# A graph layer's own-node product, moved from the node values into the PSUM sum of its edges

## The chip, the core and the metric

The kernel runs on one core of a Trainium2 chip. A core has five engines with instruction streams of their own, which wait for each other through semaphores: TensorE (PE; its weight loads are shown as PEld), VectorE (DVE), ScalarE (ACT), GpSimd (POOL) and SyncE (SP), which here only issues DMAs. Matrix products are written to PSUM; all other tiles lie in SBUF. Transfers between SBUF and DRAM are done by 16 DMA engines; SP, ACT and POOL issue them. The metric is the device time of one execution in microseconds, lower is better. Where times are compared, the median of several executions is meant.

## What is computed

Four residual steps on 6250 nodes of 256 features, each on a layer norm of x, with 106250 edges sorted by destination: a graph layer with edge attributes, an attention layer with four experts of which two count for each node, a second graph layer, and a last layer of four experts with a shared one. The change is in the second graph layer (D = 256, projection P = 128):

```python
def _L1_gnn_ref(x, edge_vals, Wp, bp, W1, b1, W2, b2, src, dst):
    MU = 2.0
    h = relu(x @ Wp.T + bp)                    # 6250 x 128: a node's own projection
    hp = h ** MU
    msgs = edge_vals[:, None] * hp[src]        # 106250 x 128
    agg = segment_sum(msgs, dst, num_segments=N)
    agg = agg ** (1.0 / MU)
    return h @ W1.T + b1 + agg @ W2.T + b2     # 6250 x 256

x = x + _L1_gnn_ref(_layernorm(x), edge_weight, ...)   # the second graph layer
x = x + _L1_ffn_ref(_layernorm(x)[None], ...)[0]       # the last experts
```

So a node gets the product of its own projection (`h @ W1.T`) and the product of the root of its edges' sum (`agg @ W2.T`). The first needs nothing but the node itself; the second needs `hp` of all its neighbours.

## The kernel before

Nodes are held in 49 tiles of 128 (a tile's number is `w` or `t`; 128 nodes lie on the 128 partitions). `x_all` and `b_all`, each 128 x 49 x 256 float32, stay in SBUF for the whole kernel: x_all is the residual stream, b_all holds what each layer needs of a node, mostly its normed values transposed (features on partitions), in two halves of 128 columns a tile. All products are float32; a product is made of two passes on PE for each factor pair, and each pass has a weight load and a matmul record.

The kernel has these stages: node products of the first graph layer (to about 270 us), its edges (to about 1675 us), the attention together with the first experts (to 3037 us), and the second graph layer's edges together with the last experts (to the end).

**The attention stage.** A loop over 80 groups of 8 columns of edges (`for k in range(NA + 5)`, line 2113) mixes several sequences by hand. In each turn POOL gathers the attention rows of group k (`fetch`), PE and DVE score, weigh and sum those of the groups before (`score`, `weigh`, `spread_out`, `add_up`), and between these parts `slot()` advances two more things: `experts1`, the first experts (products `ph` and `py`, gelu on ACT, L1607), and `steps`, in which the node values of the second graph layer are made.

`node_values(ws)` (line 1949) is a generator for two tiles at a time. It starts when their attention gates and the experts' outputs (loaded back from DRAM by L1944) are there. Its steps: sum the four experts into x_all (L1956) and take the layer norm's mean and scale (L1961 to L1970); write the normed values (ACT, L1976), and add the biases b1 + b2 to x_all (DVE, L1980); transpose them into b_all (PE L1987, ACT L1988); multiply by wpt, and relu into a tile `ht` (ACT, L1994), which is h transposed, 128 projections on the partitions by 128 nodes; then transpose `ht` back (PE, L1998) into one half of a PSUM tile `py`, multiply `ht` by w1t into the other half (L1999), square the first half on ACT (L2001), add the second to x_all on DVE (L2002), and store the square to `hp_dram` (SP, L2003). The PSUM pool `psy` has two buffers. They are shared by the transposes, the products with wpt, the back-transposes and the second products of `experts1`, so each new one waits until the last reader of the tile two before is done. After the loop, turns without attention work go on until all 49 tiles are made.

**The last stage.** The gathers of `hp` need the whole of `hp_dram`. A loop over 139 groups of six edge tiles (line 2451) does for group k: POOL gathers the rows of group k + 4 (`fetch`, six buffers `hg`), DVE makes the 96-wide selection with the edge weights (`weights_of`, L2390), PE adds the group up into the PSUM tile `pe` of the block of nodes (`add_up`, L2411). A block is four node tiles (ten such, then three of two and three of one); its tile has two buffers. When a block's last edge tile is in, `roots(b)` takes the square root of its sums on ACT (L2423), and `end_of2` is begun for one of its tiles every other turn: the product with w2t into a PSUM tile `pt` (pool `psm`, one buffer), its addition to x_all (L2229), the layer norm, a transpose into b_all (L1085, L1086) and the product with the gate's weights. When a block is through, `gates2` and `experts2` route it and run the experts; `advance` moves them by one to three steps a turn.

Weights of the last stage are loaded at its beginning, by SP, into the pool `w8`. The order in which the loops issue their work is not quite the order in which each engine runs it: the framework that builds the program schedules ready instructions of neighbouring turns into one another. For example the first loads of the last stage (L2174, 3024 us) stand on SP's queue before the last stores of hp (L2003, 3037 us). Each engine then runs its list strictly in order.

Helpers record under their own lines: a `mm` product is L1091, `transposed` L1085 and L1086, a gather L1104; the tile names tell them apart (`py<-w1t,ht` is the product that the change is about, `pt<-w2t,gt` the one of the edges).

Of the kernel before, what the change touches and what calls it, by code (L numbers as in the profile page):

```python
# [8 lines left out]
F32 = mybir.dt.float32  # L9
I32 = mybir.dt.int32  # L10
AF = mybir.ActivationFunctionType
# [5 lines left out]
P = 128  # L17
# [824 lines left out]
def kernel(ctx: ExitStack, tc: tile.TileContext, a: dict, out: bass.AP):  # L842
# [10 lines left out]
    N, D = a["x"].shape  # L853
# [63 lines left out]
    with ExitStack() as fast:  # L917
# [22 lines left out]
        def bcast_row(pool, name, ap):  # L940

            n = ap.shape[0]
            t = pool.tile([P, n], F32, name=name)
            SY.dma_start(t, bass.AP(tensor=ap.tensor, offset=ap.offset, ap=[[0, P], [1, n]]))
            return t
# [20 lines left out]
        if T1 > C1:  # L966
            V.memset(flat.bitcast(I32)[:, C1:T1], 2**24)
            n = E1 - C1 * P
# [119 lines left out]
        def mm(dst, lhs, rhs, n=2):  # L1088

            for c in range(n):  # L1090
                TE.matmul(dst, lhs(c), rhs(c), start=c == 0, stop=c == n - 1)  # L1091
# [565 lines left out]
        with (  # L1657
# [270 lines left out]
            bp = w6.tile([P, 1], F32, name="bp")  # L1928
            with nc.allow_non_contiguous_dma(reason="a bias, one element a partition"):
                SY.dma_start(bp, a["L1_gnn_bp"].rearrange("(c p) -> p c", p=P))  # L1930
            w1t = w6.tile([P, D], F32, name="w1t")
            SY.dma_start(w1t, a["L1_gnn_W1_T"])
            b1 = bcast_row(w6, "b1", a["L1_gnn_b1"])
            V.tensor_add(b1, b1, bcast_row(n6, "xn", a["L1_gnn_b2"]))
            ys = {}
            done = {"gates": 0, "loads": 0, "sums": 0, "begun": 0}

# [11 lines left out]
            def node_values(ws):  # L1949

                mv = n6.tile([P, 2, 2], F32, name="ln_mv")
                rs = n6.tile([P, 2], F32, name="ln_rs")
                off = n6.tile([P, 2], F32, name="off")
                for i, w in enumerate(ws):
                    for e in range(X):
                        V.scalar_tensor_tensor(  # L1956
                            x_all[:, w, :], ys.pop((w, e)), gate[:, w, e : e + 1], x_all[:, w, :],
                            op0=OP.mult, op1=OP.add,
                        )
                    st = n6.tile([P, 6], F32, name="ln_st")  # L1960
                    V.bn_stats(st, x_all[:, w, :])  # L1961
                    V.bn_aggr(mv[:, i, :], st)
                    V.tensor_scalar(rs[:, i : i + 1], mv[:, i, 1:2], EPS, None, op0=OP.add)
                    done["sums"] += 1
                    yield w == ws[-1]
                n = len(ws)
                SC.activation(rs[:, 0:n], rs[:, 0:n], AF.Sqrt)
                yield False
                V.reciprocal(rs[:, 0:n], rs[:, 0:n])
                V.scalar_tensor_tensor(  # L1970
                    off[:, 0:n], mv[:, 0:n, 0], -1.0, rs[:, 0:n], op0=OP.mult, op1=OP.mult
                )
                xns, hts = {}, {}
                for i, w in enumerate(ws):
                    xns[w] = n6.tile([P, D], F32, name="xn")
                    SC.activation(  # L1976
                        xns[w], x_all[:, w, :], AF.Identity, bias=off[:, i : i + 1],
                        scale=rs[:, i : i + 1],
                    )
                    V.tensor_add(x_all[:, w, :], x_all[:, w, :], b1)  # L1980
                    yield False
                begun.remove(ws)
                for w in ws:
                    pt = psy.tile([P, 2, D], F32, name="py")[:, 0, :]
                    for c in range(2):
                        at = slice(c * P, (c + 1) * P)
                        TE.transpose(pt[:, at], xns[w][:, at], ident)  # L1987
                    SC.activation(b_all[:, w, :], pt, AF.Copy)  # L1988
                    yield False
                for w in ws:  # L1990
                    ph = psy.tile([P, 2, D], F32, name="py")[:, 0, 0:P]
                    mm(ph, lambda c: wpt[:, c, :], lambda c: b_all[:, w, c * P : (c + 1) * P])
                    hts[w] = n6.tile([P, P], F32, name="ht")
                    SC.activation(hts[w], ph, AF.Relu, bias=bp)  # L1994
                    yield False
                for w in ws:
                    py = psy.tile([P, 2, D], F32, name="py")
                    TE.transpose(py[:, 0, 0:P], hts[w], ident)  # L1998
                    mm(py[:, 1, :], lambda c: hts[w], lambda c: w1t, 1)  # L1999
                    hp = n6.tile([P, PD], F32, name="hp")  # L2000
                    SC.activation(hp, py[:, 0, 0:P], AF.Square)  # L2001
                    V.tensor_add(x_all[:, w, :], x_all[:, w, :], py[:, 1, :])  # L2002
                    SY.dma_start(nodes(hp_dram)[:, w, :], hp)  # L2003
                    yield False

# [158 lines left out]
        with (  # L2164
# [7 lines left out]
        ):  # L2172
            w2t = wp.tile([P, D], F32, name="w2t")
            SY.dma_start(w2t, a["L1_gnn_W2_T"])  # L2174
            gw = load_rows(wp, "gw", a["L1_ffn_gW"])
            gb = bcast_row(wp, "gb", a["L1_ffn_gb"])
            sw1 = load_rows(wp, "sw1", a["L1_ffn_sW1"])
# [45 lines left out]
            def end_of2(b, i, root):  # L2223


                w = blocks[b][0] + i
                pm = psm.tile([P, D], F32, name="pt")
                mm(pm, lambda c: root[:, i, :], lambda c: w2t, 1)
                V.tensor_add(x_all[:, w, :], x_all[:, w, :], pm)  # L2229
                st = wk.tile([P, 6], F32, name="ln_st")  # L2230
                V.bn_stats(st, x_all[:, w, :])
                mv = wk.tile([P, 2], F32, name="ln_mv")
                V.bn_aggr(mv, st)
                rs = wk.tile([P, 1], F32, name="ln_rs")
                V.tensor_scalar(rs, mv[:, 1:2], EPS, None, op0=OP.add)
                SC.activation(rs, rs, AF.Sqrt)
                yield
                V.reciprocal(rs, rs)
                off = wk.tile([P, 1], F32, name="off")
                V.tensor_scalar(off, mv[:, 0:1], rs, -1.0, op0=OP.mult, op1=OP.mult)  # L2240
                xn = wk.tile([P, D], F32, name="xn")
                SC.activation(xn, x_all[:, w, :], AF.Identity, bias=off, scale=rs)
                yield
                transposed(psm, b_all[:, w, :], xn)
                yield
                pg = psm.tile([P, D], F32, name="pt")
                mm(pg[:, 0:NX], lambda c: b_all[:, w, c * P : (c + 1) * P], lambda c: gw[:, c, :])
                V.tensor_add(logits(b)[:, i * NX : (i + 1) * NX], pg[:, 0:NX], gb)
# [169 lines left out]

            def roots(b):
                n = blocks[b][1]  # L2420
                root = wk.tile([P, BT, P], F32, name="gt")[:, 0:n, :]
                pe = sums.pop(b)[:, 0 : n * P].rearrange("p (w k) -> p w k", k=P)
                SC.activation(root, pe, AF.Sqrt)  # L2423
                return [(b, i, root) for i in range(n)]
# [116 lines left out]
```

## Time and profile before

| | us |
|---|---|
| median of 8 runs | 4353.14 (4332.4 to 4371.82) |
| the profiled execution | 4340.81 |
| its span, first to last instruction | 4338.9 |
| attention stage in which node values are made | 2110 to 3037 |
| first gather of hp, last gather of hp | 3040.8, 4257 |
| PE, DVE, ACT, POOL busy, share of the span | 81%, 50%, 32%, 52% |
| granted TensorE clock, mean | 0.869 |

The tables of groups name a line, an engine, the tiles written and read, the shape and the count; then the busy time in us and the mean of one in ns; behind the second bar the time for which the engine sat idle just before, and what ended most of it. "x98" for a product of 49 tiles means two passes each. "Issue" is idle time in which the profile shows no wait; "remote" is a wait that ended with a signal that the profile cannot attribute. A matmul's record begins when PE takes it up, and its end is modelled, so the signal of a matmul can reach the other engines well after its recorded end. The granted clock is the share of full speed that the throttle left to PE.

### The profile page before, as it was taken

The page shows a single profiled execution, that of the slowest core. Times are in us where ns is not written, and L with a number is a line of the kernel's source. Part 1 is how long each engine was busy: PE and PEld are TensorE (multiplying, and loading weights), DVE is VectorE, ACT ScalarE, POOL GpSimd, SP SyncE. Part 2 cuts the span into 40 slices and gives each one's busy share as a digit, 9 for nine tenths or more (in the row PEclk, how much of TensorE's full clock was granted, in tenths as well). Part 3 has the DMA queues.
Part 4 walks back from the last instruction along what each step waited for, and adds up shares of the span by engine and source line. Part 5 has one row for each costly group of instructions (what it writes and reads, how often), then busy time and mean ns, then how long its engine had stood idle before and what let it go on. Part 6 is the DMA issues. An engine that isn't in the chain of part 4 may idle for free.

```text
span 4338.9 us, 57680 instructions
## 1 busy us (share of the span) xinstructions
PE 3501.4 (81%) x20063; PEld 2713.6 (63%) x20063; DVE 2185.1 (50%) x6292; ACT 1397.3 (32%) x2752; POOL 2246.3 (52%) x2367
## 2 busy tenths in 40 slices
PE   8788889998899997788888889878336866877788
PEld 3566666676666665676777777666234644555566
DVE  9788674443333333565646465656123333333445
ACT  4333333333333332333433443445001111211123
POOL 0455455555555554444544444541666666666651
PEclk9999999999999998899999999989556676766778
DMA  5455445554545443232433233333111111111210
GB/s 156 128 157 160 136 148 161 159 159 148 155 151 160 148 148 82 69 79 67 112 70 106 67 105 71 101 84 91 50 45 51 51 50 50 51 50 50 53 46 25
DMA packets 342929, 428.52 MB, mean 99 GB/s; under 512 B 139174, under 2 KB 246453, under 8 KB 342630
## 3 DMA queue, kind: packets, MB, share of 16 engines
q1 hardware_dynamic: 245174, 244.98, 19.0%
q0 software_dynamic: 89408, 178.08, 16.7%
q8 instruction: 162, 2.65, 0.3%
q10 hardware_dynamic: 8048, 1.68, 0.2%
q14 instruction: 137, 1.12, 0.1%
HBM read 382.05 MB, written 42.49 MB: 98 GB/s over the span
## 4 chain that ended last, share of the span: by engine, by line
PE 60%; another core or an unknown queue 12%; issue 11%; DVE 9%; ACT 5%; POOL 2%; DMA 2%; SPq 0%; ACTq 0%; DVEq 0%; POOLq 0%
PE ph L1091 26%; PE py L1091 9%; PE pt L1085 6%; PE pe L1443 5%; PE pe L2411 5%; PE po L1771 3%; PE pt L1091 3%; POOL hg L1104 1%; DMA rb<-low_dram 1%; PE pa L1708 1%; ACT L1607 1%; DVE order L1237 1%; ACT hh L1607 1%; DVE key L1240 1%
## 5 line engine op out<-in xcount | busy, mean ns | idle before, releaser
L1104 POOL DMA_INDIRECT yg<-y_dram,src x882 | 842.1, 955 | 804.9 <-ACT h L1422 321.1
L1104 POOL DMA_INDIRECT hg<-hp_dram,src x831 | 786.0, 946 | 451.9 <-issue 229.2
L1104 POOL DMA_INDIRECT sg<-gat_dram,src x640 | 612.7, 957 | 647.8 <-DVE px L1743 308.5
L1091 PE MATMUL ph<-w1b,et 128*128 128x256 f32 x3528 | 874.6, 389 | 32.0 <-issue 30.2
L1091 PEld LDWEIGHTS ph<-w1b,et 128*128 128x128 f32 x3528 | 654.2, 196 | 127.7 <-issue 52.3
L1417 DVE TENSOR_TENSOR yg<-ph,yg 128x512 f32<-128x512 f32 x441 | 300.1, 687 | 459.2 <-PE ph L1091 170.8
L2411 PEld LDWEIGHTS pe<-eq,hg 128*128 128x128 f32 x2036 | 373.8, 261 | 203.1 <-issue 125.5
L2411 PE MATMUL pe<-eq,hg 128*128 128x96 f32 (+15 forms) x2036 | 383.3, 341 | 139.2 <-issue 66.1
L1091 PE MATMUL py<-w,hh 128*128 128x256 f32 x1568 | 412.0, 401 | 65.2 <-ACT hh L1607 31.6
L2390 DVE TENSOR_SCALAR eq<-px,dst,ew 128x96 f32<-128x96 f32 x831 | 261.5, 369 | 324.2 <-remote 115.0
L1091 PE MATMUL ph<-b_all,w 128*128 128x256 f32 (+1 forms) x1600 | 407.0, 394 | 4.2 <-issue 4.1
L1086 ACT ACTIVATE et<-pt 128x512 f32<-128x512 f32 x441 | 259.4, 595 | 393.2 <-PE pt L1085 191.8
L1091 PEld LDWEIGHTS py<-w,hh 128*128 128x128 f32 x1568 | 297.9, 198 | 121.3 <-issue 41.0
L1422 ACT ACTIVATE h<-yg 128x512 f32<-128x512 f32 x441 | 275.7, 629 | 222.4 <-DVE yg L1417 164.4
L1091 PEld LDWEIGHTS ph<-b_all,w 128*128 128x128 f32 x1600 | 303.7, 199 | 44.3 <-issue 7.3
L1085 PE MATMUL pt<-ident,ea 128*128 128x128 f32 x1764 | 286.6, 283 | 37.6 <-issue 19.4
L1443 PE MATMUL pe<-h,eq 128*32 128x257 f32 x3168 | 256.5, 386 | 59.0 <-issue 30.6
L1607 ACT ACTIVATE hh<-ph,b 128x256 f32<-128x256 f32 (+1 forms) x400 | 166.0, 467 | 378.9 <-remote 116.8
L1085 PEld LDWEIGHTS pt<-ident,ea 128*128 128x128 f32 x1764 | 215.6, 147 | 109.4 <-issue 65.8
L1771 PE MATMUL po<-pp,B 128*128 128x240 f32 (+10 forms) x1280 | 265.5, 348 | 12.1 <-issue 8.4
L1771 PEld LDWEIGHTS po<-pp,B 128*128 128x128 f32 x1280 | 224.6, 197 | 29.0 <-issue 11.5
L1443 PEld LDWEIGHTS pe<-h,eq 128*32 128x32 f32 x3168 | 104.1, 109 | 190.2 <-issue 91.9
(331 smaller groups left out, 4324.2 us busy)
## 6 DMA issues: line engine op xcount, KB each, us to landing
ea<-in_edge_attr_dram SPq DMA_DIRECT2D x147, 768.0 KB
y<-y SPq DMA_DIRECT2D x196, 128.0 KB
w<-in_L_ffn_W_dram SPq DMA_DIRECT2D x48, 512.0 KB
y<-ys SPq DMA_DIRECT2D x96, 256.0 KB
rb<-low_dram SPq DMA_DIRECT2D x80, 256.0 KB
yg<-y_dram,src POOLq DMA_INDIRECT x882
hg<-hp_dram,src POOLq DMA_INDIRECT x831
sg<-gat_dram,src POOLq DMA_INDIRECT x640
```

What stands on the lines that cost most here:

```text
L1085: TE.transpose(pt[:, c, :], src[:, c * P : (c + 1) * P], ident)
L1086: SC.activation(dst, pt.rearrange("p c k -> p (c k)"), AF.Copy)
L1091: TE.matmul(dst, lhs(c), rhs(c), start=c == 0, stop=c == n - 1)
L1104: GP.indirect_dma_start(out=dst, out_offset=None, in_=table[0:NP, :], in_offset=IndirectOffsetOnAxis(ap=idx, axis=0),)
L1237: V.max(out=top, in_=key)
L1417: V.tensor_add(y, ph, y)
L1422: SC.activation(h[:, j : j + 2, 0:D], y, AF.Relu)
L1443: TE.matmul(sums[w][b * Q : (b + 1) * Q, :], eq[k][:, j, at], h[:, i * NT + j, :], start=g == 0 and j == NT - 1, stop=g == last_of[b] and ...
L1607: SC.activation(hidden[u][:, f, :n, :], ph[:, f - f0, :n, :], AF.Gelu, bias=b1[:, e, f : f + 1],)
L1771: TE.matmul(po.rearrange("p b v -> p (b v)"), B[:, j, :], pp[:, j, 0:n, :].rearrange("p b v -> p (b v)"), start=half == 0 and j == 0, stop ...
L2390: V.tensor_scalar(equals[k][:, j, :], lanes[:, 0:NW], dst_of[:, t : t + 1], ew[:, t : t + 1], op0=OP.is_equal, op1=OP.mult,)
L2411: TE.matmul(sums[b][:, lo - t0 * P : hi - t0 * P], hg[:, j, :], eq[:, j, lo - n0 : hi - n0], start=False, stop=after >= (t0 + n) * P,)
```

## The change

The node's own product leaves `node_values`. The relu writes h transposed into the first half of the tile's b_all, which the product with wpt has just read, where it stays. At the end of the second graph layer, `end_of2` makes one PSUM sum of two factors, b_all's first half by w1t and the edges' root by w2t, and adds that to x_all. The biases b1 + b2 are no longer added tile by tile in `node_values` but block by block in `roots`, in one wide DVE addition with the bias row broadcast over the block's tiles. w1t and the bias rows are loaded with the weights of the last stage instead of those of the attention.

```diff
@@ weights of node_values
-            w1t = w6.tile([P, D], F32, name="w1t")
-            SY.dma_start(w1t, a["L1_gnn_W1_T"])
-            b1 = bcast_row(w6, "b1", a["L1_gnn_b1"])
-            V.tensor_add(b1, b1, bcast_row(n6, "xn", a["L1_gnn_b2"]))
@@ node_values
-                xns, hts = {}, {}
+                xns = {}
...
-                    V.tensor_add(x_all[:, w, :], x_all[:, w, :], b1)
...
-                    hts[w] = n6.tile([P, P], F32, name="ht")
-                    SC.activation(hts[w], ph, AF.Relu, bias=bp)
+
+                    SC.activation(b_all[:, w, 0:P], ph, AF.Relu, bias=bp)
...
-                    TE.transpose(py[:, 0, 0:P], hts[w], ident)
-                    mm(py[:, 1, :], lambda c: hts[w], lambda c: w1t, 1)
+                    TE.transpose(py[:, 0, 0:P], b_all[:, w, 0:P], ident)
                     hp = n6.tile([P, PD], F32, name="hp")
                     SC.activation(hp, py[:, 0, 0:P], AF.Square)
-                    V.tensor_add(x_all[:, w, :], x_all[:, w, :], py[:, 1, :])
                     SY.dma_start(nodes(hp_dram)[:, w, :], hp)
@@ weights of the last stage
             SY.dma_start(w2t, a["L1_gnn_W2_T"])
+            w1t = wp.tile([P, D], F32, name="w1t")
+            SY.dma_start(w1t, a["L1_gnn_W1_T"])
+            b12 = bcast_row(wp, "b12", a["L1_gnn_b1"])
+            V.tensor_add(b12, b12, bcast_row(wp, "b2", a["L1_gnn_b2"]))
@@ end_of2
-                mm(pm, lambda c: root[:, i, :], lambda c: w2t, 1)
+                mm(
+                    pm, lambda c: (b_all[:, w, 0:P], root[:, i, :])[c],
+                    lambda c: (w1t, w2t)[c],
+                )
                 V.tensor_add(x_all[:, w, :], x_all[:, w, :], pm)
@@ roots
                 n = blocks[b][1]
+                at = slice(blocks[b][0], blocks[b][0] + n)
+                V.tensor_add(
+                    x_all[:, at, :], x_all[:, at, :],
+                    b12[:, None, :].to_broadcast([P, n, D]),
+                )
                 root = wk.tile([P, BT, P], F32, name="gt")[:, 0:n, :]
```

## The prediction

> **What bounds the kernel now.** I read the busy times in stretches first, because the change takes work out of one stage (the attention, in which the second graph layer's node values are made, 2110 to 3037 us) and puts it into another (the second graph layer with the last experts, from 3037 us on). Columns: stretch, its length, busy us of PE, PE's weight loads, DVE, ACT and POOL, then the granted clock, DMA share, GB/s.
>
> ```profile
> 2110.00:3037.00 927.00, 792.18 (x4849) 675.54 (x4849) 551.65 (x1437) 406.70 (x723) 404.00 (x420) 0.94 0.36 89
> ...
> 3178.00:4257.00 1079.00, 769.73 (x3029) 567.91 (x3030) 400.78 (x1502) 190.13 (x337) 690.08 (x730) 0.69 0.19 50
> ```
>
> The attention is PE's stage: 85% busy at a clock of 0.94. In the last stage PE is 71% busy at 0.69, and POOL issues a gather for each of 831 edge tiles; here two engines can be the bound. Second view, groups of instructions of the attention, for what the change takes away there, with PE's waits behind it; third, the same for the last stage.
>
> ```profile
> L1091 PE MATMUL py<-w1t,ht 128*128 128x256 f32 x98 | 31.1, 402 | 0.0
> ...
> L1987 PE MATMUL py<-ident,xn 128*128 128x128 f32 x98 | 21.0, 299 | 22.6 <-DVE x_all L2002 11.8 <-ACT xn L1976 4.0 <-ACT b_all L1988 3.0
> L1998 PE MATMUL py<-ident,ht 128*128 128x128 f32 x49 | 14.9, 305 | 23.0 <-DVE x_all L2002 22.0 <-issue 0.6 <-DVE ys L1623 0.3
> ...
> L2002 DVE TENSOR_TENSOR x_all<-x_all,py 128x256 f32<-128x256 f32 x49 | 20.3, 416 | 16.5 <-issue 9.2 <-ACT hp L2001 7.0
> L1980 DVE TENSOR_TENSOR x_all<-x_all,b 128x256 f32<-128x256 f32 x49 | 20.3, 419 | 10.7 <-ACT xn L1976 6.9 <-issue 3.6
> ```
>
> ```profile
> L1104 POOL DMA_INDIRECT hg<-hp_dram,src x831 | 786.0, 946 | 451.9 <-issue 229.2 <-remote 102.5 <-PE pe L2411 81.9
> ...
> L1091 PE MATMUL pt<-w2t,gt 128*128 128x256 f32 x98 | 44.0, 542 | 39.3 <-ACT b_all L1086 25.0 <-issue 13.8 <-DVE px L2248 0.3
> ```
>
> A product of 128x256 is two passes: 31.1/49 = 0.63 us a node in the attention, 44.0/49 = 0.90 us in the last stage. A gather takes 0.95 us and 0.30 of issue, 1.25 in all, 7.5 for a group of six; 831 x 1.25 = 1039 us, and POOL spends 1216 (3041 to 4257). What lies between is POOL waiting for a gather buffer that PE has yet to read. In POOL's order of time:
>
> ```profile
> 3647.26 0.95 POOL L1104 DMA_INDIRECT hg<-hp_dram,src  x1 [3.49 <-remote]
> ...
> 3654.76 0.95 POOL L1104 DMA_INDIRECT hg<-hp_dram,src  x1 [0.30 <-DMA hg<-hp_dram,src]
> ...
> 3664.47 0.95 POOL L1104 DMA_INDIRECT hg<-hp_dram,src  x1 [2.51 <-PE pt L1085]
> ...
> 3671.97 0.94 POOL L1104 DMA_INDIRECT hg<-hp_dram,src  x1 [0.30 <-DMA hg<-hp_dram,src]
> ```
>
> Each line is the first gather of a group: one group runs on at 7.5 us, the next waits some 3 us for PE. Counting along the stage, 71 of 138 groups go at POOL's pace. So PE's work counts there, but not all of it.
>
> **The change, part by part.** In the attention it removes, a node, one product (PE) and two additions on DVE; x_all is then last touched by the layer norm, and a PSUM tile `py` is free when ACT has squared it (L2001), not when DVE has added it (L2002).
>
> (a) 49 products, 31.1 us of PE. The stage is 85% PE, so I take 0.85 x 31 = 26 us off. Ends: 0, if something else were the limit, and 31.
>
> (b) PE's waits for L2002, 22.0 + 11.8 = 33.8 us. They do not all go. One of the longest:
>
> ```profile
> 2224.24 0.28 ACT L2001 ACTIVATE hp<-py 128x128 f32<-128x128 f32 x1 [0.65 <-ACT hh L1607]
> ...
> 2227.09 0.56 DVE L1725 TENSOR_TENSOR za<-pa,A 128x384 f32<-128x384 f32 x1 [4.40 <-remote]
> ...
> 2227.57 0.41 DVE L2002 TENSOR_TENSOR x_all<-x_all,py 128x256 f32<-128x256 f32 x1
> ...
> 2228.03 0.48 PE L1998 MATMUL py<-ident,ht 128*128 128x128 f32 x1 [3.21 <-DVE x_all L2002]
> ```
>
> The square is done at 2224.5, so without L2002 PE would be let on 3.2 us sooner by this tile. But DVE was itself held until 2227.09 by PE's `pa`, recorded at 2222.55 and signalled 4 us later; PE was behind its records. What is sure to go is 2228.03 - 2227.09 = 0.9 of 3.2 us, so I take 0.3 x 33.8 = 10 us. Ends 0 and 33.8. Late next is ACT's square, which waits 17.0 us in total for PE and 25.5 for its own turn.
>
> The granted clock in the three bursts of node values before 2700 us is 0.98, 0.93 and 0.95, in the quiet stretches behind them 0.95, 1.00 and 1.00: 3% lower in the mean. The Trainium skill, "TensorE: Matmul & The Clock Gate" (section "HAM oscillation — how this bites in real kernels"), says that PE gaps above some 3.4 us put PE back to half clock. By it, shorter waits would also win back that 3% of about 64 us of PE in each of some six bursts, an estimate of 12 us more, and the sum would be 29 us instead of 17; the trace agrees only loosely, so I leave it out.
>
> (c) 98 DVE additions, 20.3 + 20.3 = 40.6 us. DVE is 60% busy (551.65 of 927), so most of this is time that nobody waits for beyond (b). It is worth something where DVE paces the work: after the last edge group (2994 to 3037 us) nine nodes are still to be made, with DVE busy 28.3 of the last 37 us; 18 x 0.42 x 0.76 = 6 us. Ends 0 and 7.5. The stores of hp and the gathers behind them come that much sooner. The relu's writing into `b_all` instead of `ht` is the same activation (0.37 us) and costs nothing: the product that reads `b_all` is what it waited for already.
>
> In the last stage it adds:
>
> (d) 49 products in front of those of w2t, into the same PSUM sum, 98 passes. The same form in the same place takes 0.90 us a node, 44.0 us. The first factor is ready long before, but the PSUM tile (one buffer) is not, so it stands behind the same wait as its neighbour. Ends: 0, if POOL's gathers hide it all, and 98 x 0.70 = 69, from the slowest rows of the stage, where passes start at multiples of 0.70 us (3154.12 for a load, then 3154.83 and 3158.32 for matmuls). I take the half that falls into groups that do not keep POOL's pace: 22 us.
>
> (e) One DVE addition of the biases a block, 10 of 128x1024, 3 of 512, 3 of 256. By the rows of those sizes (L1783 1.22 us, L1623 0.69, L1980 0.42) this is 12.2 + 2.1 + 1.3 = 15.5 us on a DVE that is 37% busy here. It needs nothing that is late; queued behind it are the next group's `eq` and the node ends, once a block of some 99 us. I take 2; ends 0 and 15.5.
>
> (f) The loads of w1t and the two biases leave SP's queue early in the attention, where they delay nothing I can see, and stand in front of `gw` at 3024 us: 0.33 + 2 x 0.46 = 1.25 us of issue, with SP idle from 3027.0 to 3029.7 behind it and the stores of hp at 3029.7 to 3037.6 after that; one DVE addition (0.42) that waits for the loads. POOL's queue is passed by nothing. I take 1; ends 0 and 2.
>
> **Sum:** -26 - 10 - 6 + 22 + 2 + 1 = -17 us against the profiled execution's 4340.8. That one lies 12 us under the median of 4353.1, within the runs' 4332 to 4372; the same -17 on the median gives 4336.
>
> **The rivals.**
>
> *The gathers hide the product* (d near 0): for it, the 71 groups at 7.5 us whatever PE had to do; against it, 102.5 + 81.9 us of POOL's waits end with PE. -42 + 3 = -39, 4314 us.
>
> *PE's slow passes decide, slower:* in the node ends of the last stage each added pass takes 0.70 us and nothing hides it, because POOL, DVE and ACT all wait for PE's signal there. 98 x 0.70 = 69, sum +30, 4383 us. For it, a quarter of the chain there is put down to a queue that the profile cannot name, with PE late behind its records. Against it, the same product's mean is 0.54 a pass. It decides from (42 - 3)/98 = 0.40 us a pass net; from 0.53 it is slower beyond the noise.
>
> *The attention gives nothing back:* PE's freed time turns into waits for ACT's gelu (L1607, 27.2 us now) and for the row loads; 10 of the 42 us remain, +15, 4368 us. Against it, 85% PE.
>
> *The bias addition holds up the gathers:* DVE reads two SBUF operands for 15.5 us while POOL, which sets the pace half the time, writes gathers; if POOL stood still meanwhile, -17 + 15.5 = -2, 4351 us, no change. Of the attention's gathers, 75 begin or run beside such a DVE instruction (L1956, L1980): median 947 ns, as for the 340 others, which speaks against it. The Trainium skill, "SBUF — State Buffer" (section "Who interferes with whom"), says that DVE instructions with two SBUF inputs contend with GpSimd instructions that read SBUF; by that rule this is what would happen, and the trace does not agree.
>
> **How the numbers follow.** Forecast 0.45 (its own range -32 to -2 us), hidden 0.17, slow passes 0.27, attention gives nothing 0.06, bias addition 0.05. A change under 0.3%, 13 us, is about what a measurement of this kernel cannot tell from none. Of the forecast's 0.45 some 0.28 lies beyond it; faster 0.28 + 0.17 = 0.45, same 0.17 + 0.05 = 0.22, slower 0.27 + 0.06 = 0.33. The range takes in the hidden case with some of what is beyond it and ends at the slow passes: -46 to +31, 4307 to 4384.
>
> **What would show it.** (a, b) The stretch from the first node value to the last store of hp, 2117 to 3037 us, should be some 42 us shorter; PE's waits at L1998 and L1987 should name ACT's square for a few us where they now name L2002 for 33.8. (c) The first gather of hp should come at about 2999 us. (d) From there to the end the time should grow from 1298 to some 1323 us; the row of the product should be 196 passes and some 88 us. If POOL's waits stay at 184 us, the gathers hid it; if they grow by 60 or more, the slow passes have it. (e) The gathers beside the bias addition should stay at 947 ns. I am wrong if the attention's PE waits come back under another name, or if the last stage grows by more than the attention shrinks.

## The result, and the profile after

The changed kernel takes 4316.0 us in the median (4294.8 to 4344.8, 20 executions), the kernel before 4353.0 (4325.9 to 4380.3, 57). The ratio is 0.9922, 95% interval 0.9904 to 0.9940: 34 us less, between 26 and 42 (the medians lie 37 us apart). On another chip (the third, below), on which both kernels are 18% faster, it is 3554.2 against 3580.0, ratio 0.9928 (0.9914 to 0.9942): 26 us less. The forecast was 17 us less.

The profiled execution of the changed kernel has a span of 4312.0 us, 26.9 under that of before. Both are cut at marks that exist in both: the first gather of the attention, the first and the last square of a node value, the first gather of `hp`, the end.

| us | before | after | difference |
|---|---|---|---|
| start to the first gather of the attention | 1694.0 | 1683.6 | -10.4 |
| to the first square (first node value) | 477.8 | 485.4 | +7.6 |
| first to last square | 865.1 | 845.1 | -20.0 |
| to the first gather of `hp` | 3.9 | 3.7 | -0.2 |
| first gather of `hp` to the end | 1298.1 | 1294.2 | -3.9 |

The first row is not the change: up to there each engine runs the same work in both, and with the kernels below on the first two chips it comes out anywhere between 1677 and 1701 us, whatever they change. The second row varies likewise there, from 477.6 to 505.0 us. The row of the node values is the change. It shrank by 20 us where 42 were forecast. The last stage was to grow by 25 us and did not grow.

The busy times in stretches of the changed kernel, in the columns of the prediction (length, PE, weight loads, DVE, ACT, POOL, clock, DMA share, GB/s), for the attention with the node values and for the stretch between the first root and the last gather:

```profile
2110.00:3014.00 904.00, 768.95 (x4748) 660.01 (x4745) 525.26 (x1341) 400.66 (x717) 401.97 (x419) 0.94 0.36 91
3162.00:4234.00 1072.00, 783.95 (x3120) 573.76 (x3120) 404.34 (x1508) 189.58 (x337) 688.40 (x728) 0.72 0.19 50
```

The attention is 23 us shorter with 23 us less of PE in it, still 85% busy, and the clock still 0.94. In the last stage PE has 14 us more to do in 7 us less, and the clock went from 0.69 to 0.72. Next the groups of PE in the attention, with what ended the idle time before them:

```profile
L1091 PE MATMUL py<-w,hh 128*128 128x256 f32 x1049 | 272.2, 398 | 53.2 <-ACT hh L1607 32.3 <-issue 14.1 <-ACT hp L1995 4.8
...
L1091 PE MATMUL py<-b_all,wpt 128*128 128x128 f32 x196 | 32.8, 296 | 24.4 <-DVE ys L1623 18.2 <-issue 4.9 <-ACT b_all L1983 1.2
L1982 PE MATMUL py<-ident,xn 128*128 128x128 f32 x98 | 21.6, 309 | 27.6 <-ACT hp L1995 12.9 <-DVE ys L1623 6.5 <-ACT xn L1972 3.8
L1993 PE MATMUL py<-ident,b_all 128*128 128x128 f32 x49 | 14.1, 287 | 6.8 <-issue 2.5 <-ACT hp L1995 2.5 <-ACT b_all L1989 0.8
```

L1982, L1993 and L1995 are the L1987, L1998 and L2001 of before. The 33.8 us that PE waited for the DVE addition are gone from both transposes. In their place stand ACT's square (4.8 + 12.9 + 2.5 = 20.2 us), 9 us more for the copies of the experts' outputs (L1623: 18.2 in the row of wpt, 9.3 before) and 5 more for gelu (32.3 against 27.2). PE's idle time in this stretch was 135 us before (927.0 - 792.2) and is 135 now (904.0 - 769.0): in this pair of profiles the attention lost PE's time and no waiting. Last, PE's and POOL's rows of the last stage:

```profile
L1091 PE MATMUL pt<-w1t,b_all 128*128 128x256 f32 x97 | 43.0, 534 | 37.2 <-ACT b_all L1086 36.0 <-issue 0.9 <-DVE px L2248 0.3
...
L1091 PE MATMUL pt<-w2t,gt 128*128 128x256 f32 x98 | 38.9, 487 | 7.0 <-ACT gt L2428 7.0
```

```profile
L1104 POOL DMA_INDIRECT hg<-hp_dram,src x831 | 787.1, 947 | 446.4 <-issue 233.6 <-remote 97.8 <-PE pe L2411 75.7
```

The new product stands where its neighbour stood and has taken over its wait (36.0 us for `b_all` against 25.0). POOL's waits for PE, 97.8 + 75.7 = 173.5 us, were 184.4 before: the gathers do not wait longer for PE with its added work.

### The profile page after: what moved, and what is told of

The parts are those of the page before. It is cut to its first block, busy times and chain, and to the rows that moved or that the text cites. A ratio compares the mean times of both kernels' runs of the same rounds, so it can differ in the third digit from the quotient of the medians.

```text
span 4312.0 us, 57573 instructions
## 1 busy us (share of the span) xinstructions
PE 3493.6 (81%) x20063; PEld 2706.2 (63%) x20063; DVE 2169.9 (50%) x6210; ACT 1394.7 (32%) x2750; POOL 2248.9 (52%) x2367
## 4 chain that ended last, share of the span: by engine, by line
PE 61%; another core or an unknown queue 15%; DVE 10%; issue 8%; ACT 4%; DMA 2%; POOL 0%; SPq 0%; ACTq 0%; DVEq 0%; POOLq 0%
PE ph L1091 27%; PE py L1091 9%; PE pt L1085 7%; PE pe L1443 5%; PE pe L2411 4%; PE pt L1091 3%; PE po L1771 3%; DMA rb<-low_dram 1%; DVE key L1240 1%; PE pa L1708 1%; DVE order L1237 1%; DVE eq L2390 1%; ACT L1607 1%; DVE pp L1750 1%
## 5 line engine op out<-in xcount | busy, mean ns | idle before, releaser
L2411 PEld LDWEIGHTS pe<-eq,hg 128*128 128x128 f32 x2036 | 363.7, 254 | 222.6 <-issue 156.0
L1443 PE MATMUL pe<-h,eq 128*32 128x257 f32 x3168 | 245.9, 387 | 38.6 <-issue 15.4
L1175 DVE TENSOR_TENSOR eq<-lane,dst 128x192 f32<-128x192 f32 (+3 forms) x294 | 89.0, 340 | 231.5 <-PE pt L1085 137.3
```

The costliest lines, as they stand in the source:

```text
L1175: V.tensor_tensor(found[k], lane[:, None, lo * Q : hi * Q].to_broadcast([P, NT, n]), dst1[:, w, k, :].unsqueeze(2).to_broadcast([P, NT, n] ...
L1443: TE.matmul(sums[w][b * Q : (b + 1) * Q, :], eq[k][:, j, at], h[:, i * NT + j, :], start=g == 0 and j == NT - 1, stop=g == last_of[b] and ...
L2411: TE.matmul(sums[b][:, lo - t0 * P : hi - t0 * P], hg[:, j, :], eq[:, j, lo - n0 : hi - n0], start=False, stop=after >= (t0 + n) * P,)
```

## Experiments

The first four ran on one chip (the kernel before there: 4355.7 us), the next four on a second (4373.0), the last four on a third (3580.0). Ratios are to the kernel before on the same chip; "the stretch of the node values" is the one from the first to the last square. One execution of each was profiled. On the first two chips it took up to 15 us less or more than the median of its kernel, so a stretch that differs by some us between two profiles says little by itself. No profile of the kernel before from these two chips is on record, so their stretches are set against the 865.1 us of the table above; nor is a run of the changed kernel, so its ratio is the one of the result.

**The product left out of the last stage.**

```diff
-                mm(
-                    pm, lambda c: (b_all[:, w, 0:P], root[:, i, :])[c],
-                    lambda c: (w1t, w2t)[c],
-                )
+                mm(pm, lambda c: root[:, i, :], lambda c: w2t, 1)
```

> The changed kernel, with the nodes' own product left out of the PSUM sum of the last stage (h @ W1.T is missing from the result; everything else stays). Theory 'the gathers hide the product': the last stage, from the first gather of hp to the end, stays at 1294 us as in the changed kernel, give or take 8, and the time stays within 8 us of its 4316. Rival 'PE pays half of it' (term d of the prediction): 22 us less, 4294. Rival 'slow passes': 69 us less, 4247. The stretch before the first gather is the same in all.

Measured: ratio 0.9931 (0.9903 to 0.9958), against 0.9922 with the product. The last stage took 1309.2 us, no shorter than 1294.2 (this profiled execution lies 8 us over the median of its kernel, that of the changed kernel 2 us under). Half of the product (22 us, 0.5%) would have shown as 0.987, below the interval. The product costs nothing that can be measured.

**The product five times in the last stage.**

```diff
                 mm(
-                    pm, lambda c: (b_all[:, w, 0:P], root[:, i, :])[c],
-                    lambda c: (w1t, w2t)[c],
+                    pm, lambda c: (b_all[:, w, 0:P] if c < 5 else root[:, i, :]),
+                    lambda c: (w1t if c < 5 else w2t), 6,
                 )
```

> The changed kernel, with the own product added five times into the PSUM sum instead of once (the result holds h @ W1.T five times): 392 more passes on PE in the last stage, 176 us by the mean row of the product there (0.45 us a pass), 274 us at 0.70 us. Theory 'the gathers hide the product': PE has 288 us free of 1072 between the first root and the last gather by its records, so most of it is still hidden: less than 60 us more than the changed kernel, under 4376. Rival 'PE pays half of it': 88 us more, 4404. Rival 'slow passes': 274 us more, 4590.

Measured: ratio 0.9980 (0.9948 to 1.0012). Against the changed kernel's that is 0.0058, 25 us, for 392 passes more: 0.06 us a pass, where the prediction took 0.22 and its rival 0.70. On one and the same chip, against the kernel without the product, it is 0.0049, 21 us for 490 passes: 0.04 us a pass. POOL's waits put down to "remote" and to `pe` are 184.0 us without the product and 190.6 with five of it. The stretch between the first root and the last gather, without the product and with five of it:

```profile
3169.00:4253.00 1084.00, 779.20 (x3030) 575.68 (x3030) 402.83 (x1508) 189.65 (x337) 688.21 (x729) 0.69 0.19 50
```

```profile
3169.00:4269.00 1100.00, 820.77 (x3442) 614.62 (x3443) 411.19 (x1510) 190.12 (x337) 686.81 (x728) 0.76 0.19 49
```

PE's passes rise by 412 and its busy time by only 42 us, while its clock rises with its work: 0.69 without the product, 0.72 with it, 0.76 with five. The old passes at the higher clock and the new ones at 0.218 us each at full clock would give 779 x 0.69 / 0.76 + 412 x 0.218 / 0.76 = 826 us, an estimate near the 821 measured. So the cover is deep, and part of it goes with the clock; how much was not measured by itself. The Trainium skill, "TensorE: Matmul & The Clock Gate" (section "HAM oscillation — how this bites in real kernels"), says that PE falls to half clock after gaps of some 3.4 us. The traces do not bear out that this is what changed here. PE's matmul records have 28 gaps of more than 3.4 us in the stretch without the product, 30 in that of the changed kernel and 27 with five products, while the time at half clock fell from 670 to 600 and 522 us. On the third chip (below) the last stage of the changed kernel has no gap over 2.1 us, and is at half clock for 481 of 942 us all the same. What sets the clock in this stage stays open.

**The product made in the attention, but not read.**

```diff
-                    V.tensor_add(x_all[:, w, :], x_all[:, w, :], py[:, 1, :])
```

> The kernel before, with the own product still made in the attention but never added to x_all (L2002 taken out, so h @ W1.T is missing from the result): PE's work is all there, DVE's read of the PSUM tile is not. Theory 'the waits come back under another name': PE's 33.8 us of waits for L2002 turn into waits for ACT's square, ACT's gelu and DVE's copies of the experts' outputs; 0 to 6 us less than before, 4347 to 4353. Rival 'a third of the waits goes' (terms b and half of c of the prediction): 13 us less, 4340. Rival 'all of them go': 34 us less, 4319.

Measured: ratio 0.9946 (0.9924 to 0.9967), 24 us less (14 to 33); the stretch of the node values 855.5 us, 9.6 shorter than in the profile of before. PE's rows in it:

```profile
L1091 PE MATMUL py<-w,hh 128*128 128x256 f32 x976 | 258.8, 403 | 49.5 <-ACT hh L1607 31.0 <-issue 8.8 <-ACT hp L2001 6.9
...
L1987 PE MATMUL py<-ident,xn 128*128 128x128 f32 x94 | 20.8, 311 | 20.4 <-ACT hp L2001 10.6 <-DVE ys L1623 4.8 <-ACT xn L1976 3.1
L1998 PE MATMUL py<-ident,ht 128*128 128x128 f32 x48 | 14.3, 297 | 7.6 <-ACT hp L2001 4.5 <-issue 2.3 <-DVE ys L1623 0.3
```

PE's waits for L2002 became 22 us of waits for the square. A good part came back, but not all: the addition alone was worth 10 us by the stretch and 14 or more by the time. The theory that nothing goes falls by the time.

**No product, no addition of it.**

```diff
-                    mm(py[:, 1, :], lambda c: hts[w], lambda c: w1t, 1)
-                    V.tensor_add(x_all[:, w, :], x_all[:, w, :], py[:, 1, :])
```

> The kernel before, with the own product and its addition to x_all left out (h @ W1.T is missing from the result), the bias addition kept in node_values: what the attention gives back without PE's 31 us and without the waits for L2002. Theory 'PE's work counts, the waits come back': 20 to 26 us less than before, 4327 to 4333, and the last stage unchanged at 1298 us. Rival 'both count' (terms a, b and half of c): 39 us less, 4314. If the measured 37 us of the whole change come from here alone, it is at 4316 too.

Measured: ratio 0.9933 (0.9910 to 0.9957), 29 us less (19 to 39); the stretch 846.2, another 9.3 shorter; the last stage 1296.1 as before. So on this chip PE's share of the product, 31 us busy, is worth 9 us by the stretch, and 6 by the times.

**The product three times, not read.**

```diff
-                    mm(py[:, 1, :], lambda c: hts[w], lambda c: w1t, 1)
+                    mm(py[:, 1, :], lambda c: hts[w], lambda c: w1t, 3)
...
-                    V.tensor_add(x_all[:, w, :], x_all[:, w, :], py[:, 1, :])
```

> The kernel before, with the own product made three times in the attention (two of them more, 196 passes) and never added to x_all (h @ W1.T is missing from the result): what PE's work there is worth. The starts of two passes of this product lie 0.22 us apart, so 196 passes are 43 us of PE. Theory 'only a third of PE's time in node_values is anybody's loss', from the stretch between the first square and the last store of hp: 866 us before, 856 with the product unread, 847 without it, so 9 of 22 us; by it the stretch is some 18 us longer than with one unread product, 874, and the time 4354. Rival 'PE is the bound at 85%' (term a of the prediction): 37 us longer, 893 and 4373. Rival 'the product stands in PE's waits altogether': no longer, 856 and 4336.

Measured: ratio 1.0019 (1.0002 to 1.0036), 4381.1 us; against 0.9946 with one unread product that is 0.0073, 32 us, nearer to the rival's 37 than to 18. The stretch of 873.5 us is the 874 of the theory "only a third", though on another chip than the 856. The two do not agree: what a pass more costs here lies between 18 and 32 of the 43 us. That the product stands wholly in PE's waits is excluded on this chip itself: the next kernel, with one product and one addition more on DVE, is 26 us shorter.

**Another addition in place of the product's.**

```diff
-                    V.tensor_add(x_all[:, w, :], x_all[:, w, :], py[:, 1, :])
+                    V.tensor_add(x_all[:, w, :], x_all[:, w, :], b1)
```

> The kernel before, with the product made and left in PSUM, and L2002 adding the bias row a second time to x_all in place of the product (h @ W1.T is missing from the result, the biases are in it twice): DVE has the same number of additions of the same size as before, but none of them holds a PSUM tile. Theory 'PE waited for the tile': the gain of the unread product stays, 856 us between the first square and the last store of hp, 4336 in all. Rival 'DVE's time was the gain': 866 us and 4353, as before.

Measured: ratio 0.9960 (0.9940 to 0.9980), 17 us less, near the 24 of the unread product, which speaks for the tile. The stretch of 868.4 us, against 851.2 in the next kernel, would speak for DVE's time, but it cannot be held against it: the profiled execution here lies 15 us over its median and that one 15 us under, and by their medians the two kernels are 4 us apart the other way (4354.9 and 4358.8). How much is DVE's time stays open.

**The biases back in node_values, with their loads.**

```diff
+                    V.tensor_add(x_all[:, w, :], x_all[:, w, :], b1)
                     yield False
...
-                V.tensor_add(
-                    x_all[:, at, :], x_all[:, at, :],
-                    b12[:, None, :].to_broadcast([P, n, D]),
-                )
```

> The changed kernel, with the biases added tile by tile in node_values again and not in the roots: one of the parts of the change undone. Terms c and e of the prediction: 3 us longer in the attention, 2 us shorter in the last stage, together within 4 us of the changed kernel's 4316. Theory 'DVE is late there': the stretch between the first square and the last store of hp goes from 839 to 846 (three runs of the changed attention) to some 850, the last stage stays, 4321. Rival 'the bias addition holds up the gathers': the last stage gets 15 us shorter, 4303.

Measured: ratio 0.9971 (0.9952 to 0.9989), 13 us less than before: 21 us short of the changed kernel's gain, but on another chip. Its last stage took 1313.3 us, and that of the two kernels ahead of it, which have the last stage of before, 1315.3 and 1319.9, against 1296 to 1301 on the first chip. The first chip has a pair that differs in the place of the biases: the two kernels without any product, with the biases in `node_values` (0.9933) and in the roots (0.9931). It shows nothing like 21 us. So this called for a comparison on one chip.

**The same move carried further.** The projection is made with the nodes on the partitions, so that `hp` needs no transpose; the last stage makes it again for the own product.

```diff
-                    mm(ph, lambda c: wpt[:, c, :], lambda c: b_all[:, w, c * P : (c + 1) * P])
-
-                    SC.activation(b_all[:, w, 0:P], ph, AF.Relu, bias=bp)
...
-                    TE.transpose(py[:, 0, 0:P], b_all[:, w, 0:P], ident)
+                    mm(ph, lambda c: b_all[:, w, c * P : (c + 1) * P], lambda c: wpt[:, c, :])
...
-                    SC.activation(hp, py[:, 0, 0:P], AF.Square)
+                    V.tensor_add(hp, ph, bpr)
+                    V.scalar_tensor_tensor(hp, hp, 0.0, hp, op0=OP.max, op1=OP.mult)
...
+            def own(w):
+                ph = psm.tile([P, D], F32, name="pt")[:, 0:P]
+                mm(ph, lambda c: wpt[:, c, :], lambda c: b_all[:, w, c * P : (c + 1) * P])
+                SC.activation(b_all[:, w, 0:P], ph, AF.Relu, bias=bp)
...
+                for w in range(3 * k, min(3 * k + 3, T)):
+                    own(w)
```

> The changed kernel carried further the same way: node_values makes relu and square of the projection with the nodes on the partitions (the product's two factors exchanged), DVE adds the bias from PSUM and makes max(h, 0) * h in SBUF; the transpose of h, its relu and the square on ACT leave the attention; the last stage makes the projection again, transposed, three tiles a turn from its first turn on, 196 passes and 49 relus. Theory 'the last stage has room, and the attention's dependencies count': the waits for ACT's square (some 15 us) and 7 us of PE's starts go, 49 x 2 DVE instructions of some 0.25 us come; 840 us between first and last value become 825 to 835, the last stage stays at 1294 to 1309, 4301 to 4311. Rival 'DVE holds the tile now': PE waits for DVE as it did for L2002, 10 to 20 us longer, 4326 to 4336. Rival 'the last stage has no room for 196 more passes': 30 us longer.

Measured: ratio 0.9959 (0.9938 to 0.9979), 4353.8 us. On the same chip the change with the biases in `node_values` has 4358.8, so no gain is shown. The waits for the square are gone, as meant, but the stretch of the node values is 856.6 us, no shorter than the 851.2 there with the transposes. In it:

```profile
L1980 PE MATMUL py<-ident,xn 128*128 128x128 f32 x98 | 21.1, 302 | 27.6 <-ACT b_all L1981 19.2 <-ACT xn L1970 4.2 <-DVE hp L1987 2.5
```

PE's idle time before the first transposes is 27.6 us, the same as in the changed kernel, now for ACT's copy into `b_all`. And the first root comes 156.2 us after the first gather instead of 137.3 on the same chip. Some 7 us of that come with the additions of the biases, which that kernel does not have there (144.1 against 137.7 in the table's profiles); the other 12 fall into the turns that have the three products. The last stage took 1321.4 us against 1313.3, so it has room for most of the 196 passes, but perhaps not at any place in it.

**The change in three steps on one chip.** The four kernels are that of before, without the product, the changed one with the biases in node_values, and the changed one. Their edits are shown above.

> The kernel before once more, so that it and the next three kernels are compared on one chip, stage by stage: the runs so far came from several chips, and on one of them the last stage took 1313 to 1321 us with three kernels, on another 1296 to 1301 with two that have the same last stage. All theories: no change from before, within 0.2%; the spread of its stages is what the stages of single executions are uncertain by.

> The kernel before without the own product and its addition (h @ W1.T is missing from the result), once more: first step of a chain of three that leads to the changed kernel. Theory 'the tile that is free sooner and PE's 22 us give 19 us': 15 to 30 us less than before, all between the first and last node value. Rival 'most of the gain is in the biases': 10 us less or fewer.

> Second step of the chain: the changed kernel with the biases still in node_values; it differs from the kernel without a product in the product's 98 passes in the last stage (and in the tile that the relu writes). Theory 'the gathers hide the product': the same time as without a product, within 6 us, and the same last stage. Rival 'PE pays half of it': 22 us more. The first run of this kernel was 13 us under before, those without a product 23 to 29; if that holds on one chip, some 10 us of the product are paid.

> Third step of the chain: the changed kernel; it differs from the one before it in the biases, added block by block in the roots. Terms c and e of the prediction: within 4 us of it. Rival 'the biases' additions are worth more than they take, because node_values is where PE waits for DVE': 10 to 20 us less, between the first and last node value. Together the chain should give the 34 us measured for the whole change.

| kernel | us | ratio to before (95%) | first to last square | first gather of `hp` to the end |
|---|---|---|---|---|
| before | 3580.0 | 1.0000 (0.9991 to 1.0009) | 714.6 | 1084.6 |
| no product | 3558.6 | 0.9941 (0.9927 to 0.9954) | 689.5 | 1084.6 |
| product in the last stage | 3556.0 | 0.9933 (0.9920 to 0.9947) | 686.4 | 1083.4 |
| biases in the roots: the change | 3554.2 | 0.9928 (0.9914 to 0.9942) | 690.2 | 1081.6 |

The first step gives 21 us of the 26. Putting the product into the last stage costs nothing: 98 passes more, and the stage 1.2 us shorter. Moving the biases gives 2 us, within the intervals, and the stretch of the node values does not show it. So the 21 us that the biases seemed to be worth between two chips show on neither the first chip nor the third; on the second no pair of kernels shows what they are worth.

The waits of POOL in the last stage of the changed kernel on this chip (total, times, longest):

```profile
POOL hg L1104 <- issue: 225.8, 741, 0.3
POOL hg L1104 <- DMA hg<-hp_dram,src: 22.2, 73, 0.3
POOL hg L1104 <- DMA eb<-in_L_ffn_eb_dram: 14.9, 1, 14.9
POOL hg L1104 <- PE pe L2411: 2.7, 9, 0.3
```

POOL is held by PE at no start for longer than the 0.3 us that every start takes. All 138 groups of gathers follow each other at 7.5 us (the first at 7.8), against 70 in the first profile of the changed kernel: POOL alone sets the pace. PE has its passes beside it, as the stretches of before and of the change show:

```profile
1778.00:2492.00 714.00, 695.96 (x4536) 613.77 (x4534) 509.34 (x1334) 373.13 (x671) 373.26 (x389) 0.99 0.41 106
...
2590.00:3532.00 942.00, 809.80 (x3156) 585.62 (x3156) 414.42 (x1563) 202.49 (x360) 711.99 (x755) 0.74 0.21 59
```

```profile
1777.00:2467.00 690.00, 672.32 (x4448) 595.86 (x4444) 486.12 (x1249) 370.21 (x670) 372.59 (x389) 0.99 0.42 110
...
2565.00:3507.00 942.00, 823.32 (x3256) 604.37 (x3256) 418.94 (x1572) 204.64 (x364) 712.25 (x755) 0.74 0.21 59
```

The attention is PE's to 97%, and loses 24 us with 23.6 us of PE. The stretch from 94 us behind the first gather to the last gather is 942 us in both, with 100 passes more in the second. The waits for L2002 are missing in the attention of this chip already before the change:

```profile
L1987 PE MATMUL py<-ident,xn 128*128 128x128 f32 x94 | 19.5, 294 | 5.1 <-ACT xn L1976 4.0 <-ACT b_all L1988 0.9
L1998 PE MATMUL py<-ident,ht 128*128 128x128 f32 x49 | 14.0, 286 | 0.6 <-DVE ys L1623 0.3 <-DVE x_all L2002 0.2
```

## Why the prediction was right and wrong

The direction was right, and 4316 us lies in the range (4307 to 4384), at the rival "the gathers hide the product" (4314). That it lies in the range and so near the rival is partly luck: the forecast of -17 us was half of the 34 that came, which lie outside its own range (2 to 32), and the errors of the attention's terms and of (d) had opposite signs.

(d), the product in the last stage, +22, was the larger error: it measured nothing that shows. The step that failed is to take "the half that falls into groups that do not keep POOL's pace". That a group waits for PE does not make a pass more in PE's queue a longer wait. On the first chip four or five more products cost 0.04 to 0.06 us a pass. POOL's waits for PE ("remote" and `pe`) were 184 us before and 174 after, 184 without the product and 191 with five. On the third chip POOL does not wait for PE, and the product is free. Why the groups that do wait on the first chip wait no longer is shown only in part: PE's clock rises with the passes. The rival's 0.70 us for each added pass is excluded.

(a), PE's 31 us at 85%, -26: on the third chip the product and its addition are worth 25 us of the stretch and 21 of the time, while PE waits for L2002 there for 0.2 us only, so it is PE's time that went. The starts of a tile's two passes lie 0.218 us apart, so 98 passes are 21.4 us, and from before to the change PE's busy time in the stretch falls by 23.6; the mean of 0.40 us in the row, which gave the 31 us, runs on under the start of the next pass. The 26 was thus near the truth on this chip, though from a base that was too large. On the first chip the product without its read was worth 9 us by the stretch, a third of the 26, between two single executions.

(b), the waits for L2002, -10, with half of (c), -3: 10 us by the stretch, 24 (14 to 33) by the times on the first chip; on the third these waits are missing. (a), (b) and (c) together were forecast at 42 us; measured were 20 to 27 in the stretch (three profiles of the changed attention: 845.1, 843.9, 837.8, against 865.1) and 24 on the third chip. They were not additive: of 33.8 us of waits, 20 returned as waits for ACT's square, which the prediction named as next and then counted as "a few us". By the two profiles of the result, (b) gave nothing: PE's idle time is 135 us in both.

(c), DVE's tail after the last edge group, -6, and (e), +2: from the last addition of an edge sum to the last square it took 42.5 us before and 41.2 after, 42.9 and 39.8 on the third chip; one to three us went. Here the place of the bias addition was wrong. It was to run once a block, 99 us apart. It needs nothing but the finished x_all, and the framework moved nine of the sixteen ahead of the first gather:

```profile
3006.30 1.22 DVE L2422 TENSOR_TENSOR x_all<-x_all,b 128x1024 f32<-128x1024 f32 x1
3007.45 0.15 DVE L1965 RECIPROCAL ln_rs<-ln_rs 128x1 f32<-128x1 f32 x1
3007.52 1.20 DVE L2422 TENSOR_TENSOR x_all<-x_all,b 128x1024 f32<-128x1024 f32 x1
3008.64 0.15 DVE L1966 SCALAR_TENSOR_TENSOR off<-ln_mv,ln_rs 128x1 f32<-128x1 f32 x1
3008.71 8.03 DVE L2422 TENSOR_TENSOR x_all<-x_all,b 128x1024 f32<-128x1024 f32 x7
3016.93 2.66 DVE L2390 TENSOR_SCALAR eq<-px,dst,ew 128x96 f32<-128x96 f32 x9 [0.19 <-DVE x_all L2422]
```

The last tile's layer norm (L1965, L1966) stands twice behind an addition of 1.2 us, so up to 2.4 us of the tail's gain can have gone there, and the first selections of the last stage stand behind seven more: the first root came 144.1 us after the first gather instead of 137.7. The three profiles of the change and of the first chip with these additions have 144.1 or 144.2, those of the first two chips without them 136.5 to 137.6; on the third chip it is 94.8 against 94.4. Whether it costs something at the end is open on the first chip: of its two kernels without any product the one with these additions has the longer last stage (1309.2 us against 1296.1, single executions) and the shorter time (4327.7 against 4332.5). On the third chip no cost shows. No kernel with the additions held back was run.

The rival "the bias addition holds up the gathers" has eight gathers beside such an addition in the first profile, median 947.5 ns against 947: nothing. The Trainium skill, "SBUF — State Buffer" (section "Who interferes with whom"), says that a DVE instruction with two SBUF inputs contends with a GpSimd instruction that reads SBUF, and not with one that only writes it. The prediction applied it to gathers, which write; whether their issue counts as such a read no run here shows, and the eight cases show no contention.

Of the signs that were named: the first gather of `hp` came at 3017.8 us, not 2999; the last stage did not grow to 1323; the sum has 98 passes of w1t and 98 of w2t, some 82 us where 88 were forecast; PE's waits came back under another name, which was named as what would make the prediction wrong, and it did for (b). One reading of the profile was off by 3 us: the last gather of before starts at 4259.8 us, not at 4257, which changes no term.

## What to carry to other kernels

Work that leaves an engine's full stage was worth the distance of its starts there and not its recorded busy time (on the third chip, with PE at 97%). The waits that it held up can pass to whatever uses the same buffers next, so count them once. Where the other stage is paced by a queue of transfers, a pass more on the waiting engine can cost little, even if the profile shows that queue waiting for that engine at every other step; making the work five times measures it. And an operation with all its inputs ready goes where the scheduler likes, so look up its place on its engine before counting on it.

## What the runs showed of the hardware

The same program took 4356 us on the first chip, 4373 on the second, 4353 in the executions of the result, and 3580 on the third, where its executions lay between 3574 and 3585. The stage of the first layer's edges, the attention and the last stage were all shorter, the gathers not faster (943 ns against 946). From the page of the kernel before on the third chip, its busy times and PE's clock in 40 slices:

```profile
PE 3336.6 (93%) x20063; PEld 2650.2 (74%) x20063; DVE 2185.3 (61%) x6292; ACT 1415.2 (40%) x2752; POOL 2250.0 (63%) x2367
...
PEclk9999999999999999999999999998566777777788
```

One thing that differs is when others learn that PE is done. Four transposes and ACT's copy that waits for them, in the order of time, in the profile that the prediction used and in the one of the third chip:

```profile
999.54 0.60 PE L1085 MATMUL pt<-ident,ea 128*128 128x128 f32 x4
...
1003.08 0.60 ACT L1086 ACTIVATE et<-pt 128x512 f32<-128x512 f32 x1 [3.71 <-PE pt L1091]
```

```profile
1002.18 0.60 PE L1085 MATMUL pt<-ident,ea 128*128 128x128 f32 x4
...
1002.87 0.60 ACT L1086 ACTIVATE et<-pt 128x512 f32<-128x512 f32 x1 [1.05 <-PE pt L1085]
```

From the end in PE's record to the start of the copy it is 2.9 us in the first case and 0.1 in the second, and ACT stood idle for that time in both. Over all 441 such pairs, taken in order, the median is 2.06 us and 0.10, but the first figure has ACT's own work in it, for in most pairs ACT was still busy when the transposes ended. The copy started more than 0.3 us after both the transposes and ACT's work before it in 168 pairs of the first profile and in 5 of the second. This is the "PE behind its records" of the prediction, and it fits that the waits put down to L2002, to "remote" and to PE in POOL's row are missing on the third chip too; that it is their only source is not shown. As the program is the same, it belongs to the chip or to what ran beside it, not to the kernel. What causes it no run here shows.
